# Two Silu events instead of one per block, and a row scaling moved to GpSimd, in a state-space (SSD) layer

## The chip, the cores and the metric

The kernel runs on one core of a Trainium2 chip. The metric is the device time of one execution in microseconds (us). The engines are named as the profile names them: PE is TensorE (matmul; PEld are its weight loads), DVE is VectorE, ACT is ScalarE, POOL is GpSimd, SP is SyncE.

## The reference, cut to what matters

The reference is a chain of four layers on a tensor of 4 x 96 x 64 x 64: a Mamba layer, an SSD layer (Mamba-2), a second Mamba layer and a ConvNeXt layer. Only the second is touched. It scans the image in four orders (rows, columns, and both reversed), and for each order and image computes, with 4096 tokens, 192 inner channels, 3 heads and a state of 128:

```
zxbcdt = xs @ in_proj_w.T                   # z | x,B,C | dt
xBC    = silu(conv_b + causal conv of 4 taps over x,B,C)
dAc    = cumsum(dt * A) in a chunk of tokens
seg    = exp(dAc[s] - dAc[t]), lower triangle
y      = (C B^T * seg * dt) @ x             # inside the chunk
       + exp(dAc) * (C @ state carried in) + D * x
y      = y * silu(z)
y      = y * rsqrt(mean(y*y) + 1e-5) * gnorm_w    # RMS norm of a token
out    = y @ out_proj_w.T
```

Two things matter here. Silu is applied to x, to B and C, and to z, and it lives in another table of ScalarE than the exponentials and logarithms that everything else there needs. And each token's row of 192 values of y is multiplied by one number, its norm.

## The kernel before, in words

**Work.** Class `Ssd` goes through 64 *blocks* of 1024 tokens: 4 images, 2 orders `o` (rows, columns), 2 directions `r` (0 forward, 1 reversed), 4 blocks each. A block has 8 *chunks* of 128 tokens, so there are 512 chunks. The gates z are computed in the forward direction only and kept for the reversed one.

**Slots and points.** `run` writes out the order of all instructions by hand. One turn of its loop is a *slot* `n`; a slot does, for different chunks, all the stages of one chunk: `at(lag)` is the chunk that entered `lag` slots ago (negative: that will enter). The stages are, by line: mask of the decays (POOL L1220, lag -4), their exponentials (ACT L110, lag -3), the weights `seg` (DVE L1240, -1), the scaled inputs `xs` (POOL L1251, -2), the scores and the state (PE L1236, L1269), the decayed state (POOL L1279) and its update (DVE L1290), the output matmuls (PE L1296, L1305), the decayed output (DVE L1313) and the skip (POOL L1320), the gate (DVE L1329, L1330, lag 1), the squares (ACT L1335, lag 1), and for each pair of chunks the norm (`scale`, lag 2: a Ln and an Exp of 128x2, then two Copy of 128x192 with a scale, L1344), three transposes (`by_channels`, PE L1352, lag 4), the copy and the projection (DVE L1357, PE L1365, lag 5) and the sum (DVE L1382, lag 6). Every engine's instructions are chained in the order in which they were issued, so no engine passes a waiting instruction.

**The front.** Between the stages a slot has four points, `fill(0)` to `fill(3)`. At them the *front* of a later block is advanced: `front` puts the making of a block's x, B, C and z into a plan by *age*, where one age is one point and 4 ages are a slot. A front starts `AHEAD` slots before its block's first chunk, and the next one 32 ages later, so two fronts overlap. `XAGES` are the ages of the 8 matmul groups of x (L1092; DVE adds the bias one age later, L1101), `BCAGES` those of the 6 matmuls of B and C (L1107; ACT begins the convolution one age later with L1120, DVE adds three taps in the three ages after, L1127), `ZAGES` those of z (L1136; ACT copies one age later, L1144). All of these take their PSUM bank from one tag, `front`, with three buffers; x and B,C tiles have two buffers each. At age 31 `silu` applies Silu to the three B,C tiles (128x768, 128x768, 128x512), to the two x tiles (128x768 each) and, in the forward direction, to z (128x1536). At 40 to 42 `turned` and `kept` transpose B through PE and copy it with ACT (L1165, L1171).

**Tables.** `Tables.other` issues an activation of another table set; `back=True` has the set of Exp and Ln loaded again after it. The loads are the rows ACT_TABLE_LOAD of L115 (Silu's) and L122 (back).

**Beside it** run the preludes: for each new image and order the tokens are normalised, turned and their step sizes and decays made, a few instructions in each slot.

Of the kernel before, what the change touches and what calls it, by code (L numbers as in the profile page):

```python
# [19 lines left out]
AF = mybir.ActivationFunctionType  # L20
ALU = mybir.AluOpType
# [286 lines left out]
class Scan:  # L308
# [118 lines left out]
    def keep(self, g, i):  # L427
# [3 lines left out]
        else:  # L431
            self.fuse(g, i, xs, self.po)

    def run(self, steps, wts, front, first, later):


# [16 lines left out]
        for n in range(-LEAD, total + 26):  # L453
            start = len(traced)
            if (n + LEAD) % each == 0 and (step := (n + LEAD) // each + 1) < len(steps):
                fronts.append((n, front(step, made[step])))
# [104 lines left out]
def mamba_fusion(ctx: ExitStack, tc, k, src, dst, w):  # L561
# [99 lines left out]
    for _ in front(0, made):  # L661
        pass
# [71 lines left out]

XAGES = (0, 2, 6, 10, 14, 18, 22, 26)
BCAGES = (4, 9, 13, 18, 22, 27)
ZAGES = (1, 12, 20, 28)
AHEAD = 12  # L740

PARTS = ((0, 3), (3, 6), (6, 8))
HALF_X = QB // 2
# [2 lines left out]
class Ssd:  # L746
# [319 lines left out]
    def front(self, b, o, r, blk, made, following):  # L1066
# [5 lines left out]
        nc, k = self.nc, self.k  # L1072
# [4 lines left out]
        def at(age, what, *args):  # L1077
            plan.setdefault(age, []).append((what, args))
# [64 lines left out]
            z = self.z[blk][:, c : c + 2]  # L1143
            nc.scalar.copy(z.rearrange("p c n -> p (c n)"), held.pop(("z", c)))  # L1144

        def silu():
            for t in made["bc"]:
                k.act.other(t, t, AF.Silu, back=False)
            for half, t in enumerate(made["x"]):
                k.act.other(t, t, AF.Silu, back=(r == 1 and half == 1))  # L1150
            if r == 0:
                z = self.z[blk]
                k.act.other(z, z, AF.Silu)
            made["z"] = self.z[blk]

        def load():
            if following and following[:2] in self.ready:
                self.pk = self.stack(*following[1:])
# [14 lines left out]
        at(0, start)  # L1173
        for m, age in enumerate(XAGES):
            at(age + 1, biased, m)
        for i, age in enumerate(BCAGES):
            at(age + 1, begin, i)
            for tap in range(3):
                at(age + 2 + tap, convolve, i, tap)
        if r == 0:  # L1180
            for i, age in enumerate(ZAGES):
                at(age + 1, gated, 2 * i)
        for m, age in enumerate(XAGES):
            at(age, channels, m)
        for i, age in enumerate(BCAGES):
            at(age, project, i)
        if r == 0:
            for i, age in enumerate(ZAGES):
                at(age, gates, 2 * i)
        at(24, load)  # L1190
        at(31, silu)
        for m in (0, 4):
            at(40 + m // 4, turned, m)
            at(41 + m // 4, kept, m)
        return plan

    @staticmethod
# [139 lines left out]
    def scale(self, g):  # L1337

        nc, k = self.nc, self.k
        yz, ssq = g["pair"]["yz"], g["pair"]["ssq"]  # L1340
        k.act.exp_ln(ssq, ssq, AF.Ln, scale=1.0 / DI, bias=k.eps)
        k.act.exp_ln(ssq, ssq, AF.Exp, scale=-0.5)
        for n in range(2):
            nc.scalar.activation(yz[:, n], yz[:, n], AF.Copy, scale=ssq[:, n : n + 1])  # L1344

    def by_channels(self, g):

# [47 lines left out]
    def run(self):  # L1395
        nc = self.nc
        nblk = L // BLK
        steps = [
            (b, o, r, blk if r == 0 else nblk - 1 - blk)
            for b in range(B) for o in range(2) for r in range(2) for blk in range(nblk)  # L1400
        ]
        made = [{} for _ in steps]
        chunks = []
        for n, (b, o, r, blk) in enumerate(steps):
            for m in range(QB):
                pair = {} if m % 2 == 0 else pair
                chunks.append(dict(
                    b=b, o=o, r=r, blk=blk, m=m, c=m if r == 0 else QB - 1 - m, made=made[n], pair=pair,
                    first=(m == 0 and n % nblk == 0), last=(m == QB - 1 and n % nblk == nblk - 1),
                    second=(m % 2 == 1),  # L1410
                ))

        def front(n):
            return self.front(*steps[n], made[n], steps[n + 1] if n + 1 < len(steps) else None)

        def advance(plan, age):
            for what, args in plan.pop(age, ()):
                what(*args)


        preludes = [
            (n, self.prelude(*steps[n][:3])) for n in range(0, len(steps), nblk)
        ]
        first = preludes.pop(0)[1]

        weights = self.weights_of(self.w)
        next(first)
        next(weights)
        next(first)
        next(weights)  # L1430
        self.pk = self.stack(*steps[0][1:])
        plan = front(0)
        for age in range(48):
            advance(plan, age)
            if age % 2:
                next(first, None)
        for _ in first:
            pass
        for _ in weights:
            pass  # L1440

        engines = [e.engine for e in (nc.tensor, nc.vector, nc.scalar, nc.gpsimd)]
        traced = self.tc.nc.cur_bb.bb.instructions
        last, fronts = {}, []
        for n in range(-6, len(chunks) + 7):
            def at(lag):
                return chunks[n - lag] if 0 <= n - lag < len(chunks) else None

            began = len(traced)
            if (n + AHEAD) % QB == QB - 1 and self.pk is None and (  # L1450
                m := (n + AHEAD + 1) // QB
            ) < len(steps):
                assert steps[m][:2] in self.ready
                self.pk = self.stack(*steps[m][1:])
            if (n + AHEAD) % QB == 0 and (m := (n + AHEAD) // QB) < len(steps):
                fronts.append((4 * n, front(m)))

            def prepare():
                if n >= 0 and preludes:
                    ahead = 5 if steps[preludes[0][0]][2] == 0 else 2  # L1460
                    if n // QB >= preludes[0][0] - ahead:
                        if next(preludes[0][1], True):
                            preludes.pop(0)

            def fill(point):
                for start, plan in fronts:
                    advance(plan, 4 * n + point - start)

            prepare()
            if g := at(0):  # L1470
                self.carried(g, at(1))
            if (g := at(6)) and g["second"]:
                self.finish(g)
            if (g := at(5)) and g["second"]:
                self.turned(g)
            if g := at(1):
                self.gate(g)
            if g := at(-1):
                self.decayed(g, at(0))
            if g := at(-3):  # L1480
                self.decay(g)
            fill(0)

            if g := at(0):
                self.within(g)
            if g := at(-1):
                self.weights(g)
            if g := at(-2):
                self.inputs(g)
            if g := at(1):  # L1490
                self.square(g)
            fill(1)

            prepare()
            halves = self.bank("halves").rearrange("p (i n) -> p i n", i=2)
            if g := at(-1):
                self.state(g, halves)
            if g := at(-2):
                self.scores(g, halves)
            if g := at(0):  # L1500
                self.decayed_out(g)
            if (g := at(2)) and g["second"]:
                self.scale(g)
            fill(2)

            if (g := at(4)) and g["second"]:
                self.by_channels(g)
            if (g := at(5)) and g["second"]:
                self.project(g)
            if g := at(-1):  # L1510
                self.update(g)
            if g := at(0):
                self.skip(g)
            if g := at(-4):
                self.mask_of(g)
            if (g := at(-6)) and not g["second"]:
                self.sums_to(g)
            fill(3)
            fronts = [f for f in fronts if f[1]]

            for ins in traced[began:]:
                if ins.engine not in engines:
                    continue
                if ins.engine in last:
                    self.tc.add_manual_dep(ins, last[ins.engine].name, IN_ORDER, reason="order")
                last[ins.engine] = ins
        self.switch(None)
# [9 lines left out]
def convnext(ctx: ExitStack, tc, k, src, out, w):  # L1537
# [94 lines left out]
    ln_g, ln_b, b2, scale = (wt["vecs"][:, i : i + 1] for i in range(1, 5))  # L1632
    shift = one.tile([C, 1], F32, name="shift")
    nc.vector.tensor_tensor(shift, b2, scale, ALU.mult)

    pb = psum.tile([P, T], F32, tag="hid", name="pb", bufs=3)[:, : HID // P]
# [239 lines left out]
```

## Time and profile before

| what | value |
|---|---|
| median of 3 runs | 8655.1 us (8648.1 to 8672.4) |
| profiled execution, own time | 8648.5 us |
| its span | 8646.8 us |
| SSD layer, first to last gate (L1330) | 2786.7 to 5350.6 us of the span: 2563.9 us |
| mean granted PE clock over the span | 0.916 |
| busy in 2790 to 5350 us (2560 us): PE | 2230.8 us |
| DVE | 1847.7 us |
| ACT | 1831.1 us |
| POOL | 1609.7 us |
| table loads in the layer | 129 of 1.283 us |

The profile comes from one execution. A row of a timeline gives the start, the duration, the engine and line, the tiles as out<-in, and in brackets how long the engine was idle before it and what ended that. Rows of a window table give, for each engine, its busy time and the number of instructions, then the granted clock of PE as a share of full speed and the traffic of the DMAs. Durations on ACT and DVE overlap by about 0.1 us with the next instruction, so the distance between starts is the better price.

### The profile page before, as it was taken

What the parts mean: (1) busy time and instruction counts of PE and PEld (TensorE: products, weight loads), DVE (VectorE), ACT (ScalarE), POOL (GpSimd) and SP (SyncE); (2) the same over time, 40 slices, a digit from 0 to 9 for tenths busy, and PEclk for the clock granted to TensorE, in tenths of its full rate; (3) what the DMA queues carried; (4) which work ended last, traced back from release to release, by engine and by line L of the source; (5) the groups of instructions that cost most, each with busy time, mean ns of one, the idle gap of its engine ahead of it and who ended that gap; (6) DMA issues with size and microseconds to landing.
All of it is one profiled execution on the core that took longest, in us unless ns stands there. A gap on an engine that the chain in (4) does not pass through costs nothing. (4 is left out here: it accounts for less than half of the span.)

```text
span 8646.8 us, 111116 instructions
## 1 busy us (share of the span) xinstructions
PE 7317.8 (85%) x33944; PEld 3291.7 (38%) x33944; DVE 7340.0 (85%) x8513; ACT 5483.6 (63%) x10278; POOL 6593.1 (76%) x4333
## 2 busy tenths in 40 slices
PE   7888888888887888888888887788888888887588
PEld 1222222222223777777787786122222222221122
DVE  6999999999996777777677776899999999999786
ACT  5666666666664677777767765666666666665255
POOL 6999999999995665665665665799999999999221
PEclk8999999999997999999999988899989999998799
DMA  7999999999994223223323322998999999999553
GB/s 193 235 240 243 240 236 248 242 241 242 240 239 136 77 88 98 86 83 97 95 76 93 101 74 64 232 234 236 253 231 239 251 233 240 251 238 235 121 128 79
DMA packets 819134, 1558.45 MB, mean 180 GB/s; under 512 B 117613, under 2 KB 123529, under 8 KB 815466
## 3 DMA queue, kind: packets, MB, share of 16 engines
q1 hardware_dynamic: 815466, 1546.23, 68.9%
q8 instruction: 271, 4.44, 0.2%
q10 hardware_dynamic: 3072, 5.11, 0.2%
q14 instruction: 325, 2.66, 0.1%
HBM read 1256.10 MB, written 148.50 MB: 162 GB/s over the span
## 5 line engine op out<-in xcount | busy, mean ns | idle before, releaser
L381 POOL TENSOR_TENSOR hc<-hs,bc 128x1024 f32<-128x1024 f32 x1536 | 3604.1, 2362 | 388.1 <-DVE hs L374 318.8
L374 DVE TENSOR_TENSOR_SCAN hs<-da,carry,bs 128x1024 f32<-128x1024 f32 x816 | 1914.8, 2347 | 121.5 <-issue 47.9
L346 PE MATMUL bs<-du,seldu 64*128 64x512 f32 x4352 | 1411.6, 693 | 650.3 <-DVE hs L374 645.0
L369 DVE TENSOR_TENSOR bs<-bs,bc 128x1024 f32<-128x1024 f32 x1088 | 1319.6, 1213 | 94.9 <-PE bs L346 76.6
L110 ACT ACTIVATE da<-da,w_a 128x1024 f32<-128x1024 f32 x1088 | 1230.7, 1140 | 6.6 <-DMA da<-dd 4.3
L354 POOL TENSOR_TENSOR du<-du,bc 128x1024 f32<-128x1024 f32 x448 | 1060.9, 2368 | 27.5 <-DMA da<-dd 27.5
L346 PEld LDWEIGHTS bs<-du,seldu 64*128 64x128 f32 x4352 | 395.5, 199 | 1624.4 <-issue 1141.9
L1127 DVE SCALAR_TENSOR_TENSOR bc<-front,taps,bc 128x384 f32<-128x384 f32 (+1 forms) x1152 | 651.5, 566 | 302.7 <-ACT bc L1120 302.2
L395 PE MATMUL py<-hc,selsum 128*32 128x512 f32 x6144 | 835.7, 614 | 37.2 <-DVE y L412 24.3
L110 ACT ACTIVATE bs<-da,w_a 128x1024 f32<-128x1024 f32 x448 | 500.2, 1116 | 539.0 <-DVE hs L374 269.1
L196 PE MATMUL pu<-h,w_conv 96*64 96x512 f32 (+1 forms) x3072 | 823.4, 656 | 7.7 <-ACT h L185 7.2
L1320 POOL TENSOR_TENSOR y<-y,xs 128x192 f32<-128x192 f32 x496 | 293.5, 592 | 690.2 <-DVE y L1313 602.6
L374 DVE TENSOR_TENSOR_SCAN hs<-bs,carry,du 128x1024 f32<-128x1024 f32 x336 | 781.3, 2325 | 0.6 <-ACT bs L110 0.5
L110 ACT ACTIVATE seg<-seg,ndac 128x128 f32<-128x128 f32 x1536 | 502.8, 390 | 298.7 <-POOL seg L1220 294.6
L374 DVE TENSOR_TENSOR_SCAN hs<-da,bs 128x1024 f32<-128x1024 f32 x272 | 622.1, 2287 | 40.2 <-issue 16.5
L1092 PE MATMUL front<-sconv,pk 128*128 128x192 f32 x3072 | 638.7, 348 | 6.7 <-ACT dtrow L938 5.7
L1251 POOL TENSOR_TENSOR xs<-x,coef 128x576 f32<-128x576 f32 x512 | 590.2, 1153 | 20.3 <-DVE y L1329 20.2
L1092 PEld LDWEIGHTS front<-sconv,pk 128*128 128x128 f32 x3072 | 541.2, 207 | 12.3 <-ACT dtrow L938 6.9
L1220 POOL TENSOR_TENSOR seg<-dr,mask 128x384 f32<-128x384 f32 x512 | 511.5, 999 | 8.8 <-DMA dr<-rows 8.8
L1668 DVE SCALAR_TENSOR_TENSOR acc<-strips,kern,acc 128x512 f32<-128x512 f32 x504 | 424.2, 843 | 53.1 <-ACT acc L1658 36.6
L202 ACT COPY x<-pu 128x512 f32<-128x512 f32 x192 | 111.7, 582 | 515.4 <-PE pu L196 515.4
L425 PE MATMUL po<-y,w_out 64*96 64x512 f32 x768 | 437.9, 667 | 0.0
(225 smaller groups left out, 12877.1 us busy)
## 6 DMA issues: line engine op xcount, KB each, us to landing
da<-dd SPq DMA_DIRECT2D x3072, 256.0 KB
du<-dg SPq DMA_DIRECT2D x896, 256.0 KB
dr<-rows SPq DMA_DIRECT2D x256, 384.0 KB
bc<-rows SPq DMA_DIRECT2D x256, 256.0 KB
dd<-delta SPq DMA_DIRECT2D x192, 256.0 KB
dg<-du SPq DMA_DIRECT2D x192, 256.0 KB
pk<-xn SPq DMA_DIRECT2D x128, 384.0 KB
pk<-xn SPq DMA_DIRECT2D x128, 256.0 KB
```

The costliest lines, as they stand in the source:

```text
L110: self.last = self.scalar.activation(out, in_, func, **kw)
L196: nc.tensor.matmul(pu[HALFP * i : HALFP * (i + 1)], lhsT=wt["conv"][:kk, tap, D0[j] : D0[j] + HALFP], rhs=h[:kk, ds(i * T + tap, T)], star ...
L346: nc.tensor.matmul(g["bs"][:, i], lhsT=self.sel["du"][rows, g["half"], g["q"]], rhs=g["made"]["du"][rows, g["j"]], start=True, stop=True,)
L354: self.tc.nc.gpsimd.tensor_tensor(g["du"], g["du"], self.b_or_c(g, 0), ALU.mult)
L369: nc.vector.tensor_tensor(dbx, dbx, self.b_or_c(g, 0), ALU.mult)
L374: nc.vector.tensor_tensor_scan(out, da, dbx, init, ALU.mult, ALU.add)
L381: nc.gpsimd.tensor_tensor(g["hc"], hs, self.b_or_c(g, 1), ALU.mult)
L395: nc.tensor.matmul(py[ds(HALFP * i + QUART * x["half"], QUART)], lhsT=self.sel["sum"][:, q], rhs=x["hc"][:, i], start=(q == 0), stop=(q == ...
L1092: nc.tensor.matmul(p, lhsT=held["pk"][:, i, ds(order[m] * Q, Q)], rhs=self.conv[:, i], start=(i == 0), stop=(i == 2),)
L1127: nc.vector.scalar_tensor_tensor(out, shifts[tap], self.taps[:, q, tap : tap + 1], out, ALU.mult, ALU.add)
L1220: self.nc.gpsimd.tensor_tensor(seg, g["pair"]["dr"][:, ds(g["c"] % 2 * NH, NH)], self.mask[:, g["r"]].to_broadcast([P, NH, Q]), ALU.add,)
L1251: self.nc.gpsimd.tensor_tensor(xs, x.to_broadcast([P, 3, NH, HD]), coef.to_broadcast([P, 3, NH, HD]), ALU.mult)
```

## The change

The one event `silu` becomes two, `silu_x` (x, and z in the forward direction) at age 33 and `silu_bc` (B and C) at age 45; each loads the table and loads it back. `AHEAD` grows from 12 to 15 slots, the ages of x, B and C, z and of the transposes of B are dealt anew, the loop starts two slots earlier, and the first front is issued over 60 ages. The two Copy activations that scale a pair of chunks leave ACT; a new stage `scaled` has GpSimd do it with two `tensor_scalar`, one slot later (lag 3, between the inputs and the squares), still ahead of the transposes at lag 4. With `AHEAD` 15 a front's age 0 falls into a slot whose `n` is 1 modulo 8.

```diff
-XAGES = (0, 2, 6, 10, 14, 18, 22, 26)
-BCAGES = (4, 9, 13, 18, 22, 27)
-ZAGES = (1, 12, 20, 28)
-AHEAD = 12
+XAGES = (2, 6, 10, 14, 18, 22, 26, 30)
+BCAGES = (19, 23, 27, 31, 37, 41)
+ZAGES = (8, 11, 24, 28)
+AHEAD = 15
...
-        def silu():
-            for t in made["bc"]:
-                k.act.other(t, t, AF.Silu, back=False)
-            for half, t in enumerate(made["x"]):
-                k.act.other(t, t, AF.Silu, back=(r == 1 and half == 1))
-            if r == 0:
-                z = self.z[blk]
-                k.act.other(z, z, AF.Silu)
+        def silu(tiles):
+            for n, t in enumerate(tiles):
+                k.act.other(t, t, AF.Silu, back=(n == len(tiles) - 1))
+
+        def silu_x():
             made["z"] = self.z[blk]
+            silu(made["x"] + [made["z"]] * (r == 0))
+
+        def silu_bc():
+            silu(made["bc"])
...
-        at(31, silu)
+        at(33, silu_x)
+        at(45, silu_bc)
         for m in (0, 4):
-            at(40 + m // 4, turned, m)
-            at(41 + m // 4, kept, m)
+            at(53 + m // 4, kept, m)
+            at(52 + m // 4, turned, m)
...
         k.act.exp_ln(ssq, ssq, AF.Ln, scale=1.0 / DI, bias=k.eps)
         k.act.exp_ln(ssq, ssq, AF.Exp, scale=-0.5)
+
+    def scaled(self, g):
+
+        yz, ssq = g["pair"]["yz"], g["pair"]["ssq"]
         for n in range(2):
-            nc.scalar.activation(yz[:, n], yz[:, n], AF.Copy, scale=ssq[:, n : n + 1])
+            self.nc.gpsimd.tensor_scalar(yz[:, n], yz[:, n], ssq[:, n : n + 1], None, ALU.mult)
...
-        for age in range(48):
+        for age in range(60):
...
-        for n in range(-6, len(chunks) + 7):
+        for n in range(-8, len(chunks) + 7):
...
+            if (g := at(3)) and g["second"]:
+                self.scaled(g)
             if g := at(1):
                 self.square(g)
```

## The prediction

> **What bounds the kernel now.** I read the slices first, to find the layer and to see whether one engine fills it.
>
> ```profile
> PE   7888888888887888888888887788888888887588
> DVE  6999999999996777777677776899999999999786
> ACT  5666666666664677777767765666666666665255
> POOL 6999999999995665665665665799999999999221
> PEclk8999999999997999999999988899989999998799
> ```
>
> Slices 13 to 25 are the SSD layer: PE at 8 tenths is the fullest, DVE, ACT and POOL sit at 5 to 7. Nothing is full over the whole stage, so the question is when PE stands still. Next, the start times of the 512 gates (L1330) give the length of every slot. The slots of a forward block from 3732.20 us on are 9.29, 7.16, 4.75, 3.12, 4.08, 3.42, 4.21 and 3.61 us. Two slots in each block are long. Over the first 62 blocks the six other slots have a mean of 4.07 us, and the two long ones exceed twice that by 8.0 us on average (median 8.66): 496 us of the 2564 are this excess. What happens there is in ACT's timeline:
>
> ```profile
> 3728.00 1.28 ACT L115 ACT_TABLE_LOAD   x1
> 3729.30 2.10 ACT L115 ACTIVATE bc<-bc 128x768 f32<-128x768 f32 x3
> 3731.30 1.56 ACT L115 ACTIVATE x<-x 128x768 f32<-128x768 f32 x2
> 3732.76 1.47 ACT L115 ACTIVATE z<-z 128x1536 f32<-128x1536 f32 x1
> 3734.24 1.28 ACT L122 ACT_TABLE_LOAD   x1
> 3735.53 0.98 ACT L110 ACTIVATE seg<-seg,ndac 128x128 f32<-128x128 f32 x3
> ```
>
> The event holds ACT for 7.53 us, nearly two slots, and all that ACT owes the others queues behind it. DVE and PE tell when they missed it:
>
> ```profile
> 3739.05 0.62 DVE L1127 SCALAR_TENSOR_TENSOR bc<-front,taps,bc 128x384 f32<-128x384 f32 x1 [5.55 <-ACT bc L1120]
> ...
> 3746.53 0.36 DVE L1101 TENSOR_TENSOR x<-front,xbias 128x192 f32<-128x192 f32 x1 [3.43 <-PE front L1092]
> ```
>
> DVE waits 5.55 us for the next front's L1120. The second wait, on PE, has another cause, which the windows show:
>
> ```profile
> 3734.00:3736.00 2.00, 1.27 (x9) 0.95 (x7) 0.00 (x0) 1.98 (x4) 2.00 (x3) 1.00 0.00 0
> 3736.00:3738.00 2.00, 0.72 (x7) 0.72 (x8) 0.00 (x0) 2.00 (x8) 0.25 (x1) 1.00 0.68 189
> 3738.00:3740.00 2.00, 0.55 (x5) 0.41 (x4) 0.95 (x3) 1.94 (x8) 0.00 (x0) 1.00 0.02 8
> ...
> 3744.00:3746.00 2.00, 2.00 (x9) 2.00 (x8) 0.00 (x0) 1.62 (x4) 1.90 (x2) 0.50 0.00 0
> ...
> 3760.00:3764.00 4.00, 4.00 (x31) 3.94 (x30) 3.97 (x12) 1.33 (x5) 3.32 (x5) 1.00 0.46 141
> ```
>
> After the columns of PE, PEld, DVE, ACT and POOL comes the granted clock. PE idles in 3734 to 3740, then runs at 0.50 for 6.83 us, and does half the work there: another 3.4 us gone. 5.55 + 3.4 is about the 8.66 of a typical block. In the dense part (last line) PE and DVE are both full, so 4 us a slot is the pace without the event.
>
> **What the Trainium skill says.** "ScalarE: Activation LUTs", What ACT_TABLE_LOAD costs: 1283 ns a load plus about 1380 ns of drain. The load agrees (1283 ns, x129), but the drain isn't seen: from 3728.00 to the first Silu are 1.30 us, so I pay 1.29. "TensorE: Matmul & The Clock Gate", Part 1: a window of about 3.4 us of idle halves the clock. The trace agrees: 0.50 for 6.83 us after such a hole, and the four blocks whose excess is only 3.4 us (the fifth of each image) have no low clock at all. "Perfetto Trace Analysis", Optimizing Scalar/DVE Operations: where these engines aren't saturated but cause bubbles, breaking up instructions may let work finish sooner; ACT, 1831 of 2560 us busy, is that case.
>
> **The change part by part.** Prices are distances between starts.
>
> *Scaling.* Out of ACT go 512 Copy of 0.40 us (L1344, two in 0.80): 205 us. Into ACT come 128 - 64 = 64 more pairs of loads: 128 x 1.29 = 165 us. ACT's sum falls by 40 us, which is off the path by itself. Into POOL come 512 tensor_scalar of 128x192, which no row shows. From below: one input only, "GPSIMD Engine Reference", 4.1 Engine selection, calls one-input work roughly line rate and two-input about twice that, so an estimate of half of L1320, 0.3 us. From above: L1320 itself, two inputs of the same size, 0.59 us. I take 0.45. POOL's slot today is 0.55 + 0.96 + 0.48 + 1.13 = 3.12 us of 4.07, so 0.95 us is free and the addition is hidden; if that cover were gone it would cost at most 512 x 0.59 = 302 us. `scaled` waits for ACT's Exp of the slot before, and behind it on POOL stand the skip (DVE's gate waits for it) and the next mask (ACT's exponentials).
>
> *Two events.* By the trace, B and C take 2.00 us of the 7.53, z 1.46. So `silu_x` is 5.53 us forward and 4.07 reversed, `silu_bc` 4.59. I follow ACT's order with one point = 1.02 us (4.07 / 4).
> `silu_x` stands at point 1 of the front's slot 0, behind the exponentials (0.90), an L1120 (0.57) and a square (0.55): start at 2.0, end at 7.5. Then the norm's Ln and Exp (0.56), exponentials (0.90), square (0.55) and the L1120 of age 38 (0.57): done at 10.1. DVE asks for it at age 39, that is point 7, at 7.1: **3.0 us late**, reversed 1.5. POOL's `scaled` (point 5, behind decayed state and inputs at about 5.6) gets its norm at 8.1, 2.5 us late; this runs beside DVE's delay and is not added.
> `silu_bc` at point 13 waits for DVE's last tap there, start 13.7, end 18.3; then 0.90, 0.55, 0.56, 0.90 and L1120 0.57: 21.8 for a need at 21.4. The copy of B behind it frees PE's bank at 22.9 for a need at 22.4: **0.5 us late**.
> Sum per block: 3.5 forward, 2.0 reversed, mean 2.75. The same tally for the kernel before gives, from the event's start to the end of L1120, 7.53 + 1.8 + 1.1 + 0.36 + 0.57 = 11.4 us, against 11.05 measured, so the method holds there. The half clock: PE's idle is then about 3 us at most, near the bound, so I charge a quarter of 3.4 us, 0.85. Excess 3.6 instead of 8.0: (8.0 - 3.6) x 62 = 273 us gained.
>
> *Dealing, buffers, start.* The same matmuls and vector work, moved: no sum changes. No DMA is added; the load of the next front's tokens on SP stays at age 24 and its first user moves from 8 to 10 points behind, so it gets easier. One margin shrinks: with 15 slots of lead the x tile's first write (age 3) comes two points after POOL's last read of its old tile (age 1); POOL's inputs ended 1.3 us behind the gate in the dense slots, so it holds, barely. Three more slots of lead at the start with front work alone: +8 us, an estimate from some 3 us a slot.
>
> **Sum**: 8648.5 - 273 + 8 = 8383.5 for an execution like the profiled one. The median of the runs is 6.6 us above that one; 8390 for the median.
>
> **The rivals.** *Slack swallows it*: ACT runs ahead, the clock never falls, excess about 1 us: 7.0 x 62 = 434 less, 8655 - 434 + 8 = 8229. For it: no engine but PE is above 1850 of 2560 us. PE permits it: 2231 us minus half of the 447 us at low clock is about 2007 us. Against: Ln and Exp stand right behind `silu_x`.
> *Two holes instead of one* (slower): each event empties PE long enough to halve the clock, 3.4 us twice a block: 3.5 + 6.8 = 10.3 and 2.0 + 6.8 = 8.8, mean 9.55 against 8.0, so 1.55 x 62 = 96 more, with the start 8655 + 104 = 8759. The place is PE at points 8 to 11 and at 22; it decides from a mean excess above 8.0 us a block. For it: two table switches remain on the same queue. Against: the tally's second hole is only 0.5 us.
> *POOL becomes the pace*: a tensor_scalar of 1 us, or the x tile's margin gone, makes a slot of about 4.45 us: 0.38 x 512 = 195 of the gain lost, 8390 + 195 = 8585. For it: POOL rises to 3.6 of 4.07 us.
>
> **How the numbers follow.** Forecast 0.58, slack 0.20, POOL 0.11, two holes 0.11. About 0.3% (26 us) is what a measurement of this kernel can tell from no change. Of POOL's case 0.04 falls within that. So faster 0.85, same 0.04, slower 0.11. The range runs from 8210, just past the slack case, to 8640, past POOL's case; outside lie the two holes and a little below.
>
> **What would show it.** Right: in the profile after, two ACT_TABLE_LOAD pairs a block, DVE's wait for L1120 down from 5.5 to about 3 us, POOL waiting about 2.5 us for ACT's norm, PEclk at 9 in the stage, slots outside the events still near 4.1 us. Wrong: a clock of 0.50 after each event (two holes), or POOL busy through every slot with DVE waiting for it (POOL's pace), or L1101 waiting for POOL's inputs.

## The result, and the profile after

The change makes the kernel faster, by 105 us and not by the 265 of the forecast.

| | before | after |
|---|---|---|
| median (lowest to highest) | 8651.6 us (8645.7 to 8672.4, 4 runs) | 8546.5 us (8534.3 to 8554.6, 4 runs) |
| ratio, 95% interval | | 0.9873 (0.9852 to 0.9894) |
| profiled execution, own time; span | 8648.5; 8646.8 us | 8550.7; 8548.9 us |
| first gate | 2786.7 us | 2798.3 us |
| first to last gate | 2563.9 us | 2452.9 us |
| six shorter slots of a block, mean ("six") | 4.073 us | 4.294 us |
| the two longest, beyond twice that ("excess") | 8.00 us | 4.35 us |
| PE at half clock between those gates ("half clock") | 447 us | 259 us |
| busy between those gates, PE / DVE / ACT / POOL | 2235 / 1851 / 1834 / 1612 us | 2196 / 1864 / 1798 / 1982 us |

A slot is counted from its gate (L1330 before, L1332 after) to the next. The two rows on slots are means over the first 62 blocks, as in the prediction. The slices of the profile after, in the same order as before:

```profile
PE   7888888888886988988988897888888888887588
DVE  6999999999996777777777775999999999999786
ACT  5666666666664777777777775666666666665255
POOL 6999999999995787887877886899999999999221
PEclk8999999999997999999999998899999999998799
```

In slices 14 to 24 POOL has gone from 5 and 6 tenths to 7 and 8 (1982 of 2453 us, 81%, where it was 63% before); ACT, whose sum fell, still shows 7 throughout because the stage is shorter. The clock row, in tenths, is too coarse to show the fall at half clock that the table has.

The steps of the tally can be read in one forward block, the one whose gates run from 3759.19 us. ACT's timeline:

```profile
3760.09 1.28 ACT L115 ACT_TABLE_LOAD   x1
3761.39 1.58 ACT L115 ACTIVATE x<-x 128x768 f32<-128x768 f32 x2
3762.87 1.47 ACT L115 ACTIVATE z<-z 128x1536 f32<-128x1536 f32 x1
3764.34 1.28 ACT L122 ACT_TABLE_LOAD   x1
3765.64 0.30 ACT L110 ACTIVATE ssq<-ssq,eps 128x2 f32<-128x2 f32 x1
```

From the load at 3760.09 to the Ln behind it are 5.55 us; the prediction had 5.53. What DVE and then POOL missed meanwhile (in brackets the idle time before the instruction, and what ended it):

```profile
3767.87 0.48 DVE L1127 SCALAR_TENSOR_TENSOR bc<-front,taps,bc 128x256 f32<-128x256 f32 x1 [3.38 <-ACT bc L1120]
```
```profile
3766.26 1.51 POOL L1350 TENSOR_SCALAR yz<-yz,ssq 128x192 f32<-128x192 f32 x2 [2.25 <-ACT ssq L110]
3767.73 0.59 POOL L1322 TENSOR_TENSOR y<-y,xs 128x192 f32<-128x192 f32 x1
```

DVE is 3.38 us late (forecast 3.0), POOL 2.25 (forecast 2.5). The first POOL row holds a number that was not forecast: its two instructions take 1.47 us up to the start of the row behind them, so one `tensor_scalar` takes 0.74, where the prediction paid 0.45. The groups by form give its duration over the whole layer (count | busy us, mean ns | idle before and its releasers):

```profile
L1350 POOL TENSOR_SCALAR yz<-yz,ssq 128x192 f32<-128x192 f32 x512 | 385.9, 767 | 93.5 <-ACT ssq L110 82.9 <-PE y L1307 10.2
L1322 POOL TENSOR_TENSOR y<-y,xs 128x192 f32<-128x192 f32 x496 | 294.5, 594 | 362.5 <-DVE y L1315 361.9
```

The one-input row is slower than the two-input row of the same size. Last, the waits in 2900 to 5100 us (total us, times, longest):

```profile
ACT seg L110 <- POOL seg L1222: 444.0, 292, 3.6
POOL y L1322 <- DVE y L1315: 332.0, 230, 6.5
DVE bc L1127 <- ACT bc L1120: 225.5, 168, 3.5
...
POOL yz L1350 <- ACT ssq L110: 77.2, 51, 2.5
PEld front L1092 <- ACT bt L1172: 55.1, 46, 2.8
```

Before, in the same window:

```profile
POOL y L1320 <- DVE y L1313: 522.2, 261, 7.1
DVE bc L1127 <- ACT bc L1120: 248.9, 86, 6.1
ACT seg L110 <- POOL seg L1220: 247.9, 181, 3.0
```

POOL waited 522 us for DVE's decayed output, and ACT 248 us for POOL's mask. Now POOL waits less for DVE and ACT waits 196 us more for POOL: POOL has moved towards the head of the chain. DVE's wait for L1120 is little smaller in sum (249 us before), but it is cut in twice as many pieces (168 for 86), none over 3.5 us where the longest was 6.1.

**The slots by place.** The first slot of a block here is the one in which a front has its age 0. Their means are 4.45, **6.11**, 4.52, 4.65, 3.49, **6.58**, 4.64 and 4.27 us. The second pays for `silu_x` (DVE waits 2.47 us a block there for L1120, on average over both directions; the forecast's mean of 3.0 and 1.5 is 2.25). The sixth has no event: `silu_bc` runs two slots earlier, about 3776.15 to 3780.85 in this block. What it has are the transposes of B. In the next block PE's and ACT's timelines read:

```profile
3821.13 0.38 PE L1238 MATMUL halves<-bc 128*128 128x128 f32 x2
3823.85 1.70 PE L1092 MATMUL front<-sconv,pk 128*128 128x192 f32 x6 [2.34 <-ACT bt L1172]
```
```profile
3823.23 1.05 ACT L1172 COPY bt<-front 128x512 f32<-128x512 f32 x2
3825.98 0.69 ACT L110 ACTIVATE seg<-seg,ndac 128x128 f32<-128x128 f32 x2 [1.70 <-POOL seg L1222]
```

PE has no free `front` bank until ACT has copied B out of one. The windows around it (columns as before: PE, PEld, DVE, ACT, POOL, granted clock) show the price:

```profile
3820.00:3824.00 4.00, 1.35 (x9) 1.17 (x10) 2.79 (x8) 3.97 (x15) 4.00 (x6) 1.00 0.32 88
3824.00:3828.00 4.00, 4.00 (x16) 3.65 (x17) 2.28 (x6) 1.27 (x4) 3.52 (x5) 0.57 0.03 11
```

PE falls to 1.35 of 4 us, with ACT and POOL both full, and the clock is 0.57 in the window behind. This is one of the longer waits: over the layer PE waits 55.3 us in 45 pieces for this copy, about 0.9 us a block.

### The profile page after: what moved, and what is told of

Its sections match the earlier page's. It is cut to its first block, busy times and chain, and to the rows that moved or that the text cites. A ratio compares the mean times of both kernels' runs of the same rounds, so it can differ in the third digit from the quotient of the medians.

```text
span 8548.9 us, 110994 instructions
## 1 busy us (share of the span) xinstructions
PE 7284.9 (85%) x33944; PEld 3265.7 (38%) x33944; DVE 7355.1 (86%) x8513; ACT 5450.9 (64%) x9894; POOL 6965.6 (81%) x4845
## 5 line engine op out<-in xcount | busy, mean ns | idle before, releaser
L1092 PE MATMUL front<-sconv,pk 128*128 128x192 f32 x3072 | 642.1, 349 | 115.3 <-ACT bt L1172 55.3
L1253 POOL TENSOR_TENSOR xs<-x,coef 128x576 f32<-128x576 f32 x512 | 591.7, 1156 | 14.3 <-DVE y L1331 13.6
L1350 POOL TENSOR_SCALAR yz<-yz,ssq 128x192 f32<-128x192 f32 x512 | 385.9, 767 | 93.5 <-ACT ssq L110 82.9
```

Of the source, the lines that this page charges most:

```text
L1092: nc.tensor.matmul(p, lhsT=held["pk"][:, i, ds(order[m] * Q, Q)], rhs=self.conv[:, i], start=(i == 0), stop=(i == 2),)
L1253: self.nc.gpsimd.tensor_tensor(xs, x.to_broadcast([P, 3, NH, HD]), coef.to_broadcast([P, 3, NH, HD]), ALU.mult)
```

## The experiments

All are the kernel after with a small edit, except where said. "To after" is the difference of the ratios to before, times 8655 us, since the kernel before itself gave 8651.6 to 8663.2 us in these comparisons. "Six", "excess" and "half clock" are as in the table above, from one profile each.

A difference to after carries the intervals of both ratios, 22 to 27 us either way. So e8 and e9 cannot be told from the kernel after by their times, and e7, e12 and e13 barely. The stretches outside the two gates vary from profile to profile too: the first gate of the kernels other than before lies between 2784.8 and 2807.5 us, and from the last gate to the end they take 3288.2 to 3310.9 us. Most of the times also lie outside the ranges of both theories that stood for them; e3, e6 and e15 fell into one, and e11 kept its step from e10. The slots and the waits therefore carry the argument more than the times do.

| kernel | median us | ratio to before (95%) | to after, us | six | excess | half clock us |
|---|---|---|---|---|---|---|
| after | 8546.5 | 0.9873 (0.9852 to 0.9894) | 0 | 4.294 | 4.35 | 259 |
| e1_scale_on_act | 8615.2 | 0.9946 (0.9932 to 0.9961) | +63 | 4.220 | 6.30 | 314 |
| e2_scale_moved_alone | 8655.1 | 0.9994 (0.9981 to 1.0007) | +105 | 4.294 | 6.26 | 461 |
| e3_one_tensor | 8508.7 | 0.9821 (0.9806 to 0.9836) | -45 | 4.176 | 4.66 | 222 |
| e4_no_scaling | 8490.6 | 0.9805 (0.9789 to 0.9821) | -59 | 4.134 | 4.85 | 181 |
| e5_x_no_tables | 8400.9 | 0.9690 (0.9667 to 0.9713) | -158 | 4.058 | 3.70 | 126 |
| e6_bc_no_tables | 8499.3 | 0.9811 (0.9794 to 0.9829) | -54 | 4.249 | 4.26 | 280 |
| e7_bt_later | 8584.0 | 0.9905 (0.9887 to 0.9923) | +28 | 4.422 | 4.13 | 345 |
| e8_bt_later_one_tensor | 8529.9 | 0.9848 (0.9829 to 0.9866) | -22 | 4.319 | 3.97 | 263 |
| e9_bc_off_point0 | 8528.3 | 0.9855 (0.9834 to 0.9876) | -16 | 4.253 | 4.31 | 304 |
| e10_none_behind_x | 8459.1 | 0.9771 (0.9750 to 0.9792) | -88 | 4.190 | 3.55 | 137 |
| e11_none_behind_one_tensor | 8418.3 | 0.9728 (0.9709 to 0.9747) | -126 | 4.036 | 4.33 | 133 |
| e12_x_behind_norm | 8523.0 | 0.9843 (0.9828 to 0.9857) | -26 | 4.232 | 4.52 | 208 |
| e13_no_transposes | 8523.8 | 0.9847 (0.9832 to 0.9862) | -23 | 4.323 | 3.72 | 328 |
| e14_no_scaling_bc_no_tables | 8417.4 | 0.9723 (0.9705 to 0.9741) | -130 | 4.087 | 4.14 | 143 |
| e15_z_spread | 8427.5 | 0.9729 (0.9709 to 0.9748) | -125 | 4.028 | 4.39 | 140 |

### Each part alone

**e1_scale_on_act**: the new dealing and the two events together, with the scaling left on ACT in its old place, at lag 2 straight behind the norm.

```diff
-            self.nc.gpsimd.tensor_scalar(yz[:, n], yz[:, n], ssq[:, n : n + 1], None, ALU.mult)
+            nc.scalar.activation(yz[:, n], yz[:, n], AF.Copy, scale=ssq[:, n : n + 1])
...
-            if (g := at(3)) and g["second"]:
-                self.scaled(g)
...
                 self.scale(g)
+                self.scaled(g) 
```

> The changed kernel with the two scalings of a pair left on ACT (Copy, 0.40 us each, right behind the norm's Exp); the two Silu events and the new dealing stay. Theory POOL: the kernel after lost about 110 us because the six slots of a block outside the two long ones went from 4.07 to 4.29 us, and that is the 2 x 0.74 us of scaling in POOL's slot. Then these slots return to about 4.1 us (-100 us), and 0.8 us more behind silu_x in one slot of each block costs up to 0.8 x 62 = 50: about 8495 us (8450 to 8520), clearly faster than 8546. Theory DEALING: the slots are longer because x, B, C and z are dealt anew and three PSUM banks of the front collide; POOL had room. Then the six slots stay at 4.3 us, ACT is the fuller engine, and the time is 8546 to 8600.

**e2_scale_moved_alone**: the kernel before with the scaling alone changed.

```diff
-            nc.scalar.activation(yz[:, n], yz[:, n], AF.Copy, scale=ssq[:, n : n + 1])
+            self.nc.gpsimd.tensor_scalar(yz[:, n], yz[:, n], ssq[:, n : n + 1], None, ALU.mult)
...
+            if (g := at(3)) and g["second"]:
+                self.scaled(g)
```

> The kernel before with one part of the change alone: the scaling on GpSimd a slot later; one Silu event and the old ages. Theory POOL: ACT has 0.8 us less ahead of the event in each block (-50 us), but the six slots grow by 0.2 us as in the kernel after (+110): 8700 us (8660 to 8740), slower than before. Theory DEALING: the slots don't grow, only the 0.8 us is gained: about 8600 us.

The dealing with its two events, without the move, is worth 0.54% (47 us; no run separates the two events from the new ages), the move alone nothing that can be told from zero (5 us; its interval has 1 in it), both together 110 of 8655. So some 58 us, 25 either way, belong to neither part by itself. The slots say why. In e2 the excess falls from 8.00 to 6.26 us, as ACT has less to catch up with behind its event, and the six other slots rise from 4.073 to 4.294: 1.74 x 62 = 108 us won, 0.221 x 8 x 62 = 110 us lost. In e1 the six are 4.220 and the excess is 6.30, so that the move from there to the kernel after wins 1.95 x 62 = 121 us of excess and loses only 0.074 x 8 x 62 = 37 us of pace. In e1 the Copies, 0.80 us a pair, stand in ACT's queue behind the Silu events, ahead of what DVE and PE wait for. Two waits of e1, which were 225.5 and 55.1 us in the kernel after:

```profile
DVE bc L1127 <- ACT bc L1120: 306.3, 168, 4.4
...
PEld front L1092 <- ACT bt L1172: 82.0, 44, 3.6
```

How the move lengthens the six other slots is seen by place. The scaling stands in every second slot, both instructions together. POOL's wait for DVE's decayed output in the four slots of a block that hold it falls from 3.89 us before to 0.41 in e2, while in the four others it goes from 5.73 to 6.35. POOL has hardly any free time left where the scaling stands, and in e2 DVE waits for POOL's skip, which before was 4.7 us in all:

```profile
DVE y L1329 <- POOL y L1320: 62.8, 67, 2.1
```

A rival is that DVE's own work became slower while POOL does more. It did not: the gate's last multiplication takes 358 ns before and 357 after, and DVE's busy sum between the gates is 1851 and 1864 us.

### What the scaling costs on POOL

**e3_one_tensor**: one instruction for the pair.

```diff
-        for n in range(2):
-            self.nc.gpsimd.tensor_scalar(yz[:, n], yz[:, n], ssq[:, n : n + 1], None, ALU.mult)
+        self.nc.gpsimd.tensor_tensor(
+            yz, yz, ssq[:, :, None].to_broadcast([P, 2, DI]), ALU.mult
+        )
```

> The changed kernel with the two tensor_scalar of 128x192 (0.77 us each, 1.48 a pair) replaced by one GpSimd tensor_tensor of 128x384 whose second input is the norm, repeated along the row; the mask on the same engine has that size and form at 1.00 us. Theory POOL: 0.5 us less in every second slot, 256 x 0.5 = 128 us at most, half of it on the path by the share of slots that POOL paces: about 8480 us (8430 to 8520). Theory DEALING: POOL is not the pace, 8535 to 8550.

**e4_no_scaling**: `scaled` is not called, so y is not multiplied by its norm.

```diff
-            if (g := at(3)) and g["second"]:
-                self.scaled(g)
```

> The changed kernel without the scaling of y by its norm (left out altogether; the norm's Ln and Exp stay). Theory POOL: the six slots fall to 4.07 us, POOL no longer waits for the norm in the slot after silu_x: 8546 - 110 = 8435 us or less (8380 to 8450). Theory DEALING: 8530 to 8546.

The groups by form of e3:

```profile
L1349 POOL TENSOR_TENSOR yz<-yz,ssq 128x384 f32<-128x384 f32 x256 | 211.4, 826 | 93.6 <-ACT ssq L110 83.1 <-PE y L1307 10.1
```

0.83 us a pair in place of 1.5. In e3 and in e4 the pace of the six falls (from 4.294 to 4.176 and 4.134) and the excess rises a little, as the events then stand out more against a quicker pace. POOL's addition, which the prediction held to be hidden, costs 59 us, some three quarters of which one instruction in place of two gets back. With the scaling away (e4) POOL waits 4.05 us a block for the decayed output in the four slots that held it, against 0.52 in the kernel after.

### Which event holds the rest

**e5_x_no_tables** and **e6_bc_no_tables**: Exp in place of Silu on x and z, or on B and C, hence no table loads for them; durations otherwise alike.

```diff
-            silu(made["x"] + [made["z"]] * (r == 0))
+            for t in made["x"] + [made["z"]] * (r == 0):
+                k.act.exp_ln(t, t, AF.Exp)
```
```diff
-            silu(made["bc"])
+            for t in made["bc"]:
+                k.act.exp_ln(t, t, AF.Exp)
```

> The changed kernel with Exp in place of Silu for x and z: the same tiles, but the function lies in the loaded table, so the two loads of silu_x (2.57 us) fall away; silu_bc is unchanged. Theory EVENTS: the second slot of the front, 6.11 us in the kernel after against 4.29 in its neighbours, is DVE waiting for L1120 behind silu_x; 2.57 us less takes that away, 1.8 x 62 = 112: about 8435 us, and the sixth slot (6.58 us) stays. Theory POOL CIRCLE: the long slots are POOL's scaling, late mask and late exponentials, and only the part of the wait beyond POOL's work goes: 8490 to 8520.

> The changed kernel with Exp in place of Silu for B and C: silu_bc loses its two table loads (2.57 us of 4.59); silu_x is unchanged. Theory EVENTS: the sixth slot (6.58 us) falls to about 4.6, 2.0 x 62 = 124: about 8420 us. Theory BANKS: the sixth slot is long because PE has three banks out (B and C's projection and the two transposes of B) and its next x matmul waits for ACT's copy of B, which stands behind the exponentials that wait for POOL's mask; silu_bc being shorter helps only where ACT is behind on its own account: 8490 to 8520.

The loads of `silu_x` are worth 158 us, those of `silu_bc` 54, of which only 28 lie between the gates of its profile. In e5 the second slot is 3.87 us, not longer than its neighbours, and DVE's wait for L1120 in it goes from 2.47 to 0.34 us a block. The waits of e5 in 2900 to 5100 us:

```profile
ACT seg L110 <- POOL seg L1223: 513.4, 330, 3.6
...
DVE bc L1127 <- ACT bc L1120: 129.5, 160, 1.4
```

No wait for L1120 is over 1.4 us, and ACT now waits for POOL more than for anything else. In e6 the sixth slot hardly changes (6.58 to 6.37). So the second slot is `silu_x`'s, and the sixth is not made by `silu_bc`'s loads alone.

### The sixth slot

**e7_bt_later**: the transposes of B and their copies one slot later, and the last two matmul groups of z moved as well. **e8_bt_later_one_tensor**: e7 with e3's single instruction as well.

```diff
-ZAGES = (8, 11, 24, 28)
+ZAGES = (8, 11, 28, 29)
...
-            at(53 + m // 4, kept, m)
-            at(52 + m // 4, turned, m)
+            at(57 + m // 4, kept, m)
+            at(56 + m // 4, turned, m)
```

> The changed kernel with the transposes of B at ages 56 and 57 and their copies at 57 and 58 (from 52 to 54), and z's last two projections at ages 28 and 29 (from 24 and 28): no x matmul comes between a transpose and its copy with all three banks out. Theory BANKS: PE's wait for L1172 (0.9 us a block) and DVE's for L1101 in the sixth slot go, the slot falls by 1.5 to 2 us: 8546 - 105 = about 8440 us (8420 to 8470). Theory EVENTS: the sixth slot waits for L1120 behind silu_bc, no matter where the transposes stand: 8530 to 8560.

> The kernel of e7_bt_later with GpSimd's scaling as one tensor_tensor of 128x384, as in e3_one_tensor. If BANKS and POOL are two separate costs, their gains add: e3 gave about 40 us, e7 would give 105: about 8400 us, the fastest of all. If they are the same wait, seen twice, it is no better than the better of the two.

Both are slower than the kernels they edit (28 us against after, 23 against e3, each at the edge of its interval). The sixth slot falls to 5.42 us and the seventh rises to 6.27. B turned arrives late for its own user, the state's matmul, and that wait is new:

```profile
PE halves L1271 <- ACT bt L1172: 74.5, 46, 3.8
```

### What stands behind `silu_x`

**e12_x_behind_norm**: `silu_x` one point later, so that the norm's Ln and Exp are ahead of it on ACT.

```diff
-        at(33, silu_x)
+        at(34, silu_x)
```

**e9_bc_off_point0**: the fronts dealt one point off.

```diff
-XAGES = (2, 6, 10, 14, 18, 22, 26, 30)
-BCAGES = (19, 23, 27, 31, 37, 41)
-ZAGES = (8, 11, 24, 28)
+XAGES = (3, 7, 11, 15, 19, 23, 27, 31)
+BCAGES = (19, 22, 26, 30, 37, 41)
+ZAGES = (8, 10, 24, 28)
```

**e10_none_behind_x**: both of these, `silu_bc` one point later too, and the B and C matmuls dealt so that no L1120 comes soon behind `silu_x`. **e11_none_behind_one_tensor** is e10 with e3's instruction. The diff shows e10 against e9.

```diff
-BCAGES = (19, 22, 26, 30, 37, 41)
-ZAGES = (8, 10, 24, 28)
+BCAGES = (19, 22, 25, 28, 30, 42)
+ZAGES = (8, 10, 24, 29)
...
-        at(33, silu_x)
-        at(45, silu_bc)
+        at(34, silu_x)
+        at(46, silu_bc)
```

> The changed kernel with x's ages at 3, 7, ... 31 (from 2, 6, ... 30), B and C's at 19, 22, 26, 30, 37, 41 (from 19, 23, 27, 31, 37, 41) and z's at 8, 10, 24, 28 (from 8, 11, 24, 28). In the kernel after, four of the six L1120 stand at point 0 of a slot, directly behind the exponentials, which wait for the mask that POOL makes last in the slot before. Theory CIRCLE: so DVE's taps wait in every such slot for DVE L1315, POOL skip, mask, ACT exponentials, L1120, and that is what keeps the slots above 4.07 us and the sixth at 6.58 us. With three of the four at point 3, ahead of the exponentials: the waits of DVE for L1120 outside the second slot (1.0 us in the sixth) go, 1.5 to 2 us a block: about 8440 us (8420 to 8480). Theory BANKS: only PE's three banks count, and their order hardly changes: 8530 to 8560.

> As e9_bc_off_point0, but five of the six projections of B and C lie ahead of silu_x (ages 19, 22, 25, 28, 30, then 42), silu_x stands at age 34, behind the norm's Ln and Exp of that slot, silu_bc at 46, z's last projection at 29. No L1120 and no norm waits behind silu_x, so by the run without its table loads (146 us less) the second slot's 1.8 us should go too: 110 us less than e9_bc_off_point0 if that theory holds, about 8340 us (8320 to 8400). If DVE, with 12 of the 18 taps in three and a half slots, becomes the pace there, half of that: about 8400 us.

> e10_none_behind_x with GpSimd's scaling as one tensor_tensor of 128x384 (as in e3_one_tensor, which gained about 40 us). If POOL's work is a cost of its own, 30 to 40 us below e10: about 8305 us, the fastest of all.

> The changed kernel with silu_x one age later (34 for 33), so behind the norm's Ln and Exp of its slot instead of ahead of them. POOL's wait for the norm (1.29 us a block) must go. The prediction held that this wait runs beside DVE's wait for L1120 and isn't added to it: then nothing is gained, DVE's wait grows by up to 0.6 us as silu_x starts later: 8546 to 8590 us. If the two waits add, about 1.2 x 62 = 75 less: 8470.

e9 gives 16 us, within the interval and well short of what was expected of it. PE's wait for DVE leaves the second slot (0.74 us a block in the kernel after) but only moves to the third, where it is 1.31; DVE's wait for L1120 stays at 2.36 us and the second slot at 6.27. e12 takes away POOL's wait for the norm (82.9 us in the layer, 1.1 in e12) and gives 26 us, 22 either way; so that wait costs at most a little, some 0.4 us a block. e10 gives 88 us, 72 of them over e9: the second slot falls to 4.69 us, and the waits of e10 in 2900 to 5100 us show what has gone and what is next:

```profile
DVE y L1331 <- POOL y L1322: 146.2, 172, 2.5
...
DVE bc L1127 <- ACT bc L1120: 65.6, 66, 1.1
```

DVE's wait for L1120 is down from 225.5 to 65.6 us, none over 1.1. DVE's waits for POOL's skip are now larger (16.7 us in the kernel after). With the single instruction (e11) another 37 us come off, and that wait halves:

```profile
DVE y L1331 <- POOL y L1322: 78.3, 110, 1.8
```

e11 is the fastest version of the computation that was run: 8418.3 us, 0.9728 of before (0.9709 to 0.9747), 126 us under the kernel after.

### Does POOL or `silu_bc` make the sixth slot?

**e13_no_transposes**: B is not turned; the state's matmul takes it as it lies. **e14_no_scaling_bc_no_tables**: e4 and e6 together. **e15_z_spread**: e11 with the matmuls of z spread (the second diff is against e11).

```diff
-            at(53 + m // 4, kept, m)
-            at(52 + m // 4, turned, m)
+            pass
...
-            g["st"], lhsT=g["made"]["bt"][:, g["m"]], rhs=g["xs"][:, 1], start=True, stop=True
+            g["st"], lhsT=self.part_of(g["made"], g["r"], g["m"])[:, 0], rhs=g["xs"][:, 1], start=True, stop=True
```
```diff
-ZAGES = (8, 10, 24, 29)
+ZAGES = (4, 8, 12, 24)
```

> The changed kernel without the transposes of B and their copies by ACT (left out; the state's matmul reads B as it lies, a matmul of the same size). In the sixth slot PE loses 8 transposes (1.1 us at full clock), ACT two copies (1.05 us), and the front's three banks are never all out to ACT. Theory TRANSPOSES: that slot falls from 6.58 to about 4.5 us, 2.1 x 62 = 130: about 8415 us. Theory TWO CHAINS: the slot waits for L1120 behind late exponentials as before, and only PE's work goes: 0.5 to 1 us a block, 8485 to 8515.

> The changed kernel without the scaling of y (left out) and with Exp in place of Silu for B and C, so silu_bc has no table loads: e4_no_scaling and e6_bc_no_tables together. Theory TWO CHAINS: each of them alone left the other to hold the sixth slot (7.00 and 6.37 us); together it falls to about 5 us and the time to about 8370 us, more than the 56 + 47 = 103 us of the two added (8443). Theory TRANSPOSES: the slot stays above 6 us, and the time is no less than the sum gives, 8440 to 8470.

> e11_none_behind_one_tensor with z's projections at ages 4, 8, 12, 24 (from 8, 10, 24, 29): PE's front work in the last two slots of the front falls by 0.65 us in forward blocks and moves to the second and fourth slots, which are PE's lightest. If PE's uneven share makes the last two slots long (5.0 us): 0.6 us in each of 31 forward blocks, about 20 us: 8400 us. If the copy of z at age 5, now right behind silu_x, holds a bank that x needs, it is 8420 to 8450.

In e14 neither POOL's addition nor the loads of `silu_bc` are left, and the sixth slot is still 6.25 us, so those two are not what makes it. e14's 130 us stand against 59 + 54 = 113 for the two edits apart, the same within the intervals. In e13 the sixth slot is 5.35 us: the transposes make some 1.2 us of the 2.3 by which it stood above the pace, with half clock in that slot down from 1.23 to 0.60 us a block. But the whole gains only 23 us where 1.2 x 62 would be 74: the other slots, all but the fifth, lengthen by 0.1 to 0.2 us each, 0.8 us together, and the half clock over the layer rises from 259 to 328 us. Why it comes back there was not settled, nor what makes the other 1.0 us of the sixth slot. e15 is e11 within the intervals: where z's matmuls stand makes no difference there that can be told.

## Why the prediction was wrong in size

By its own sum, against the profiled execution:

| step | forecast | measured |
|---|---|---|
| excess a block | (8.0 - 3.6) x 62 = 273 us less | (8.00 - 4.35) x 62 = 226 us less |
| pace of the other slots | 0 | (4.294 - 4.073) x 8 x 62 = 110 us more |
| start | 8 us more | 11.6 us more |
| sum | 265 us less | 105 us less by this sum; 98 by the two profiled executions |

The start cannot be told from no change: in the kernels of the experiments with the same start and the same ages of x the first gate lies between 2784.8 and 2798.4 us, and before at 2786.7.

**The step that failed is "0.95 us is free and the addition is hidden".** It put the cost of the scaling on POOL at nothing, and the pace of the other slots rose by 0.221 us, 110 of the 160 us that are missing (47 more are the excess, taken up below). Two errors lie in it. The price: 0.45 us was taken, 0.59 was held to be the upper end, and it measured 0.767. The low end came from the Trainium skill, "GPSIMD Engine Reference", 4.1 Engine selection, where one-input work is roughly line rate; this case does not agree, since with a per-partition operand the one-input instruction took longer than the two-input one (0.767 against 0.594 us). And the place: the addition was spread over all slots, 0.45 in each, but it stands in every second one, both instructions together. POOL's slot there is 3.12 + 1.51 = 4.63 us, above the 4.07 it had to fit. e2 shows that price alone, with the old dealing (the six at 4.294), e4 what comes back without it in the new one (4.134): 0.160 x 8 x 62 = 79 us of pace, of which 59 show in the time, as the excess grows. The rest of the 0.221 us, some 0.06 by e4, is not POOL's scaling, and its cause stays open.

The rival "POOL becomes the pace" had the right mechanism, for most of the loss, with 4.45 us a slot and 195 us; measured were 4.294 and 110. It had a chance of 0.11 because it was made to need a `tensor_scalar` of 1 us. At 0.77, with both instructions in every second slot, it was enough. The other half of that rival, the x tile's margin, played little part: DVE's L1101 waited for POOL's inputs 13.6 us in the whole layer.

**"ACT's sum falls by 40 us, which is off the path by itself" was wrong.** Behind an event the path goes through ACT's queue, and there 0.80 us of Copy a pair are on it: leaving them there costs 63 us (e1). The sum over the layer (1834 to 1798 us) tells nothing of this.

**`silu_x`: right.** Its length, DVE's delay and POOL's delay are within 0.4 us of the tally. "This runs beside DVE's delay and is not added" is nearly right (26 us in e12). e5 shows that the second slot is not long without its two loads, and e10 that the delay is one of order: with no L1120 soon behind the event DVE's wait in that slot goes away without a shorter event.

**`silu_bc` "0.5 us late": right place, wrong size and cause.** The tally's point 22 lies in the sixth slot, and PE does wait there for the copy of B, as it said. But that slot is 6.58 - 4.29 = 2.3 us over the pace, PE's wait has a mean of 0.9 us and is 2.34 in the block shown, and the clock fell behind it. Nor are the loads of `silu_bc` what makes it: without them it is still 6.37 us (e6). The quarter of 3.4 us charged for the half clock was an average over a quantity that is there or not; half clock went from 447 to 259 us, a fall of 42%, where the charge assumed three quarters. The Trainium skill's "TensorE: Matmul & The Clock Gate", Part 1, names an idle window of about 3.4 us. The low stretch in the block shown is 3.41 us long, at 3824.50 to 3827.91, but the hole of 2.34 us ahead of it is shorter than that, and in the 3.41 us just before the clock fell PE was busy for 1.07. It was so before too: in the 3.41 us ahead of the fall at 3740.62, which the prediction counted as agreeing, PE was busy for 1.64, and it stood still at most 2.01 us at a stretch. So "about 3 us at most, near the bound" took for a bound what was none here.

**Sign and rivals.** Faster held. "Slack swallows it" fell: the excess is 4.35 us, not about 1, and is no smaller without POOL's scaling (4.85 in e4). "Two holes" fell in its sum (excess 4.35, not 9.55), though there is a second hole where it put one, at point 22; the transposes of B make about half of it (e13), the loads of `silu_bc` little (e6).

## What to carry to other kernels

Work given to an engine with idle time has to fit the slot in which it stands, together with what the engine already does there, not the mean slot; an engine that others wait for each turn has no free time beyond that. In a queue kept in order, the cost of a long event is set by what is needed soon behind it: deal that ahead of it first (e10: 88 us with no instruction removed), then see what a shorter queue is worth. Two edits that relieve one queue are measured together and apart, since here one gave 47 us, the other nothing, and both 110.

## What was not expected of the hardware

- GpSimd's `tensor_scalar` on 128x192 with a 128x1 operand took 0.767 us, a `tensor_tensor` of two full inputs of that size 0.594. One `tensor_tensor` of 128x384 whose second input is repeated along its row took 0.826, about half of two `tensor_scalar`.
- Taking transposes away from PE (e13) raised the time at half clock, 259 to 328 us in one profile each; what makes the new holes was not shown.
- PE need not stand idle for 3.41 us to lose its clock. Every stretch at half clock between the gates of before and after lasted 3.41, 6.83 or 10.24 us, and in the 3.41 us ahead of each of the 52 stretches of the kernel after PE was busy for 0.71 to 2.21 us.
